# Layer 1's second aggregation as four 64x64 tiles in two PSUM banks

## The chip, the cores and the metric

The kernel runs on one core of a Trainium2 chip. The metric is the device time of one execution in microseconds (us), taken as the median of several runs; lower is better. Where a profile is used, it is one execution recorded by the hardware profiler, and its span goes from the first to the last instruction.

## The reference

There are 128 graphs of 128 nodes with 256 features (`x`, 128x128x256) and one adjacency matrix each (`adj`). Two layers follow each other, each with a layer norm and a ReLU in front and a residual sum behind.

Layer 0 mixes the nodes of a graph by two convolutions and by messages over `exp(-dist)`, and joins them in a GRU cell (the gates r, z and n). It is most of the work.

Layer 1 is a graph convolution on the first 25 nodes of each graph. Five groups of these nodes (25, 9, 7, 6 and 6 of them, 53 rows in all, with repeats) each have their own weights:

```
A    = adj[group] + I;  norm = D^-1/2 A D^-1/2
h    = relu(norm @ (x_g @ W1) + b1)       # 256 -> 512
out  = relu(norm @ (h @ W2) + b2)         # 512 -> 256
fused[group] += softmax(fusion_w)[g] * out
```

What is computed here in the second line is called the second aggregation: `norm @ (h W2)` for the 53 rows of a graph, where `norm` is block diagonal over the five groups. All of it is in float32.

## The kernel before, in words

**Stages.** The kernel has three parts in time. Stage A (normalising, transposing, the first convolution, a Fourier transform) and stage B (products per frequency) alternate in two batches up to 680 us. From there stage C does the gates of layer 0 for four graphs at a time (32 steps `q`), and layer 1 runs beside it, behind it by some steps. At the end layer 1's last blocks run alone.

**Order.** Nothing is scheduled by a compiler. The stages are generators that emit instructions and then yield a pair: TensorE time in us that the emitted step is thought to cost, and a delay before the next step of this generator. `Order.run` picks the next generator from the lanes by these numbers and the lanes' weights. So a cost written in a `yield` decides what stands beside what on every engine. Layer 1's lane has two programs at once with weight 0.2: `prepare(blk)` and `block(blk)`, for eight blocks of 16 graphs.

**prepare(blk).** It loads the 25x25 corners of 16 adjacency matrices as `aj` (L960, on SyncE's queue), lets POOL add the identity into `b1` (L965, eight operations), lets VectorE sum the degrees (L970, five reductions), and builds on TensorE and VectorE the normalised matrices: `ac`, 128 partitions by 8 pairs by 64, where partitions 0 to 63 hold one graph of a pair and 64 to 127 the other (L976, L978, L997, L999, L1002, L1003). From `ac` it forms `r4`, which applies the first aggregation (matmul `pr`, L1007, and four copies by quarters of the partitions, L1011). Positions in `r4` and in `aj` fix which of the four graphs of a group sits in which tile.

**block(blk).** For each of its four groups `q` of four graphs, a matmul with `r4` aggregates (L1027). Then `first(g)` and `second(g)` multiply by W1 and W2 (L1044, L1053) into `yz`. The tail of the block has three functions per `q`: `turn(q)` transposes `yz` to `zt` (L1075, copied by ScalarE, L1079), with 64 partitions for each of two graphs and two such pairs side by side; `gather(q)` does the second aggregation (L1087), adds the bias on VectorE (L1089) and applies ReLU on ScalarE (L1090); `fuse(q)` sums the groups with their weights (L1096), adds to the residual (L1098) and stores (L1101, in the last block L1105). They follow each other in a fixed order: turn 0, 1, 2, gather 0, turn 3, gather 1, gather 2, fuse 0, gather 3, fuse 1, 2, 3.

**The gather's tiles.** A matmul with a contraction over 64 rows and 64 output partitions uses a quarter of the 128x128 array. `ac[rows, ...]` is the weight, `zt[rows, a]` the moving operand. Where the operands start (partition 0 or 64) decides the rows of the array, and where the output starts decides the columns. Before, graph `s` of a pair takes rows 64s and also columns 64s: two tiles of the array on its diagonal, for pair `a` = 0 and then for `a` = 1. Both write the one bank `pg2`.

**PSUM.** The pool `ptmp` has five banks and serves layer 1 and the small products of stage C in turn; a tile takes the bank of the tile five allocations earlier and waits until that one has been read. The pool `pgat` has three, for the large products.

**Stage C, as far as needed.** `turn_back` forms `xc` (L720, L723), and VectorE its sums `tc` (L586). The products of the gates are L738 (into `wrz`, `wn`, `wh` tiles); ScalarE copies the first into `u2` (L772); VectorE empties others (L798, L809, L838, L846, L854) and the output transposes (L887); POOL does the last mix (L864 to L867).

Of the kernel before, what the change touches and what calls it, by code (L numbers as in the profile page):

```python
# [9 lines left out]
FP = mybir.dt.float32  # L10
AF = mybir.ActivationFunctionType
ALU = mybir.AluOpType
# [3 lines left out]
B, N, D = 128, 128, 256  # L16
# [3 lines left out]
P = 128  # L20
GB = 4
# [9 lines left out]
SB = 16  # L31
# [7 lines left out]
NR = sum(SIZES)  # L39
NN = 25  # L40
RP = 64
WIDE = 32
# [50 lines left out]
def _constants():  # L93

    row_node = [n for g in GROUPS for n in g]
    row_group = [i for i, g in enumerate(GROUPS) for _ in g]
    fwd, inv, tap = _fourier()
    parts = {
        "ident": np.eye(P),
        "mhalf": np.full((P, 8), -0.5),  # L100
        "fwd": fwd, "tap": tap, "inv": inv,
        "ones2": np.kron(np.eye(2), np.ones((RP, RP))),
        "et": np.zeros((P, 2 * RP)),
        "same": np.zeros((P, RP)),
        "diag": np.zeros((P, RP)),
        "e4": np.zeros((P, P)),
        "s2": np.zeros((P, 2 * WIDE)),
        "grp": np.zeros((P, NG)),
        "sgrp": np.zeros((P, 2 * NG)),
        "grpt": np.zeros((P, P)),  # L110
        "sel": np.zeros((P, P)),
        "emb": np.zeros((P, 12)),
    }

    roles = {0: [(2, 2, 0), (0, 0, 1), (1, 1, 0), (0, 0, 1)],
             1: [(0, 0, -1), (0, 0, 1), (1, 1, 0), (1, 1, 0)],
             2: [(1, 1, 0), (1, 1, 0), (0, 0, -1), (0, 0, 1)]}
    for j in range(GB):
        for role, factors in roles.items():
            for ch in range(3):  # L120
                k = WIDE * j + 3 * role + ch
                parts["sel"][ch, k] = 1
                parts["emb"][k] = np.array(factors).T.reshape(-1)
    for r, (n, g) in enumerate(zip(row_node, row_group)):
        for s in range(2):
            k = s * RP + r
            parts["et"][n, k] = 1
            parts["same"][k, [i for i in range(NR) if row_group[i] == g]] = 1
            parts["diag"][k, r] = 1
            for j in (s, s + 2):  # L130
                parts["e4"][k, j * WIDE + n] = 1
            parts["s2"][k, s * WIDE + n] = 1
            parts["grp"][k, g] = 1
            parts["sgrp"][k, s * NG + g] = 1
            parts["grpt"][g, k] = 1
    at, o = {}, 0
    for name, a in parts.items():
        at[name] = (o, o + a.shape[1])
        o += a.shape[1]
    return np.concatenate(list(parts.values()), 1).astype(np.float32), at  # L140
# [67 lines left out]
def kernel(ctx: ExitStack, tc: tile.TileContext, x, adj, consts, vecs, w_se, conv1_w,  # L208
                    conv2_w, w_msg, b_msg, w_ih, w_hh, W1, W2, b2, fusion_w, out):
    nc = tc.nc  # L210
# [7 lines left out]
    ptmp = ctx.enter_context(tc.tile_pool(name="ptmp", bufs=5, space=PSUM))  # L218
# [38 lines left out]
    s2w = cp.tile([P, 2 * WIDE], FP, name="s2w")  # L257
# [106 lines left out]
    lab, turn = ExitStack(), []  # L364
# [588 lines left out]
    def prepare(blk):  # L953

        while not (blk - 1 in P_DONE and blk - 2 in {-2, *B1_DONE}):
            yield 0.0, 1.0
        pool, pool2, b1 = S["pool"], S["pool2"], S["b1"]
        ac, r4 = S["ac"][blk % 2], S["r4"][blk % 2]
        aj = pool.tile([NN, SB, NN], FP, tag="dd", name=f"aj{blk}")
        nc.sync.dma_start(out=aj, in_=adj[blk * SB:(blk + 1) * SB, :NN, :NN]  # L960
                          .rearrange("b n m -> n b m"))
        yield 0.0, 4.0

        for r, n, w in _runs():
            nc.gpsimd.tensor_tensor(b1[:, :, r:r + w], aj[:, :, n:n + w],  # L965
                                    ident[:NN, None, n:n + w].to_broadcast([NN, SB, w]),
                                    ALU.add)
        dg = pool2.tile([NN, SB, NG], FP, tag="dg", name=f"dg{blk}")
        for g in range(NG):
            nc.vector.reduce_sum(dg[:, :, g], b1[:, :, OFFS[g]:OFFS[g] + SIZES[g]],  # L970
                                 axis=mybir.AxisListType.X)
        yield 0.0, 7.0

        pa = ptmp.tile([P, SB // 2, RP], FP, tag="tmp", name=f"pa{blk}")
        for p in range(SB // 2):
            nc.tensor.matmul(pa[:, p], b1[:, 2 * p:2 * p + 2, :].rearrange("n s r -> n (s r)"),  # L976
                             c("et")[:NN, :RP], start=True, stop=True)
        nc.vector.tensor_mul(ac, pa, c("same")[:, None, :].to_broadcast([P, SB // 2, RP]))  # L978

        pdg = ptmp.tile([P, SB // 2, 2, NG], FP, tag="tmp", name=f"pdg{blk}")  # L980
        nc.tensor.matmul(pdg.rearrange("p a s g -> p (a s g)"), c("et")[:NN],
                         dg.rearrange("n b g -> n (b g)"), start=True, stop=True)
        dsel = pool.tile([P, SB // 2, 2 * NG], FP, tag="dsel", name=f"dsel{blk}")
        nc.vector.tensor_mul(dsel, pdg.rearrange("p a s g -> p a (s g)"),
                             c("sgrp")[:, None, :].to_broadcast([P, SB // 2, 2 * NG]))
        dm = pool.tile([P, SB // 2], FP, tag="dm", name=f"dm{blk}")
        zo = pool.tile([P, SB // 2], FP, tag="zo", name=f"zo{blk}")
        nc.vector.reduce_sum(dm, dsel, axis=mybir.AxisListType.X)
        nc.vector.tensor_scalar(zo, dm, 0.0, None, op0=ALU.is_equal)
        nc.vector.tensor_add(dm, zo, dm)  # L990
        nc.gpsimd.tensor_tensor(dm, dm, c("mhalf"), ALU.pow)
        nc.gpsimd.tensor_mul(zo, zo, dm)
        nc.gpsimd.tensor_sub(dm, dm, zo)
        yield 2.0, 7.0

        dd = pool.tile([P, SB // 2, RP], FP, tag="dd", name=f"dd{blk}")
        nc.vector.tensor_mul(dd, c("diag")[:, None, :].to_broadcast([P, SB // 2, RP]),  # L997
                             dm[:, :, None].to_broadcast([P, SB // 2, RP]))
        nc.vector.tensor_mul(ac, ac, dm[:, :, None].to_broadcast([P, SB // 2, RP]))  # L999
        yield 0.0, 6.0  # L1000
        pg = ptmp.tile([P, SB // 2, RP], FP, tag="tmp", name=f"pg{blk}")
        nc.tensor.matmul(pg, c("ones2"), dd, start=True, stop=True)  # L1002
        nc.vector.tensor_mul(ac, ac, pg)  # L1003
        yield 0.9, 3.0

        pr4 = ptmp.tile([P, QS, 2, RP], FP, tag="tmp", name=f"pr4{blk}")
        nc.tensor.matmul(pr4.rearrange("p q a r -> p (q a) r"), c("e4"), ac,  # L1007
                         start=True, stop=True)
        for j in range(GB):
            s = slice(j * WIDE, (j + 1) * WIDE)  # L1010
            nc.vector.tensor_copy(r4[s, :, j, :], pr4[s, :, j // 2, :NR])  # L1011
        yield 0.9, 1.0
        P_DONE.add(blk)

    def block(blk):
# [64 lines left out]

        def gather(q):
            zt = zts[q]
            pg2 = ptmp.tile([P, 2, D], FP, tag="tmp", name=f"pg2{blk}_{q}")
            for a in range(2):
                for s in range(2):
                    rows = slice(s * RP, (s + 1) * RP)
                    nc.tensor.matmul(pg2[rows, a], ac[rows, 2 * q + a], zt[rows, a],  # L1087
                                     start=True, stop=True)
            nc.vector.tensor_tensor(zt, pg2, b2row[:, None, :].to_broadcast([P, 2, D]), ALU.add)  # L1089
            nc.scalar.activation(zt, zt, AF.Relu)  # L1090

        def fuse(q):
            zt = zts.pop(q)
            pf = ptmp.tile([P, D], FP, tag="tmp", name=f"pfu{blk}_{q}")
            for a in range(2):
                nc.tensor.matmul(pf[a * 2 * WIDE:(a + 1) * 2 * WIDE], s2w, zt[:, a],  # L1096
                                 start=True, stop=True)
            nc.vector.tensor_add(x1[:, q], x1[:, q], pf)  # L1098
            b0 = blk * SB + q * GB
            if blk < NBLK - 1:  # L1100
                nc.gpsimd.dma_start(out=out[b0:b0 + GB, :WIDE], in_=x1[:, q])  # L1101
                return
            for j in range(GB):
                eng = nc.scalar if q == QS - 1 and j % 2 else nc.sync
                eng.dma_start(out=out[b0 + j, :WIDE], in_=x1[j * WIDE:(j + 1) * WIDE, q])  # L1105

        for what, q in ((turn, 0), (turn, 1), (turn, 2), (gather, 0), (turn, 3), (gather, 1),
                        (gather, 2), (fuse, 0), (gather, 3), (fuse, 1), (fuse, 2), (fuse, 3)):
            what(q)
            if (what, q) == (gather, QS - 1):  # L1110
                B1_DONE.add(blk)
            yield {turn: 0.45, gather: 0.9, fuse: 0.5}[what], 0.5
        F_DONE.add(blk)


# [70 lines left out]
```

## Time and profile before

| what | value |
|---|---|
| median of 3 runs | 2072.65 us |
| lowest and highest run | 2071.14 and 2078.92 us |
| profiled execution, first to last instruction | 2070.6 us |
| mean granted TensorE clock | 0.993 |
| TensorE matmuls busy | 2032.3 us |
| VectorE / ScalarE / POOL busy | 1161.9 / 712.7 / 730.1 us |
| gather matmuls (L1087), 256 records | 34.2 us busy |
| gather additions (L1089), 32 | 689 ns each |

The profile gives no time of its own beyond the span. A float32 matmul leaves two records, one for each of its passes; a transpose leaves one. Records of matmuls overlap[...]: the distance from one start to the next says what a matmul costs, not the length of a record. In the groups, the number after "|" is the time in which at least one record of the group runs, then the mean length of one in ns, then the idle time of the engine before it and who ended it. In the timeline, "x8" is eight records that follow each other, and a bracket says how long the engine was idle before and what it waited for.

### The profile page before, as it was taken

What the parts mean: (1) busy time and instruction counts of PE and PEld (TensorE: products, weight loads), DVE (VectorE), ACT (ScalarE), POOL (GpSimd) and SP (SyncE); (2) the same over time, 40 slices, a digit from 0 to 9 for tenths busy, and PEclk for the clock granted to TensorE, in tenths of its full rate; (3) what the DMA queues carried; (4) which work ended last, traced back from release to release, by engine and by line L of the source; (5) the groups of instructions that cost most, each with busy time, mean ns of one, the idle gap of its engine ahead of it and who ended that gap; (6) DMA issues with size and microseconds to landing.
All of it is one profiled execution on the core that took longest, in us unless ns stands there. A gap on an engine that the chain in (4) does not pass through costs nothing.

```text
span 2070.6 us, 31082 instructions
## 1 busy us (share of the span) xinstructions
PE 2032.3 (98%) x11316; PEld 1649.4 (80%) x11316; DVE 1161.9 (56%) x2711; ACT 712.7 (34%) x1611; POOL 730.1 (35%) x898
## 2 busy tenths in 40 slices
PE   7998999999999999999999999999999999999998
PEld 5667888888888788788778787878787888778875
DVE  6774445874433556646654654566456655654542
ACT  4663223444222444233222332232332323323333
POOL 3552665333664123322422243233223323233230
PEclk9999999999999999899999999999999999999999
DMA  9997788545777444223323232322232332323121
GB/s 215 294 284 237 259 273 269 180 153 202 254 257 249 142 125 139 75 75 90 85 62 90 84 83 76 106 79 75 82 93 72 81 96 80 86 77 102 35 74 52
DMA packets 190135, 281.72 MB, mean 136 GB/s; under 512 B 23625, under 2 KB 143374, under 8 KB 189982
## 3 DMA queue, kind: packets, MB, share of 16 engines
q1 hardware_dynamic: 156942, 185.46, 31.4%
q0 software_dynamic: 32656, 93.98, 14.3%
q8 instruction: 90, 1.47, 0.3%
q14 instruction: 63, 0.52, 0.1%
q10 hardware_dynamic: 384, 0.28, 0.1%
HBM read 187.34 MB, written 92.27 MB: 135 GB/s over the span
## 4 chain that ended last, share of the span: by engine, by line
PE 93%; DVE 2%; DMA 2%; POOL 1%; issue 1%; ACT 1%; SPq 0%; DVEq 0%; POOLq 0%; ACTq 0%
PE p L738 42%; PE pa L526 7%; PE pm L630 5%; PE ph L1044 5%; PE pz L1053 5%; PE pc L421 4%; PE pb L526 3%; PE pi L703 3%; PE pf L432 3%; PE px L656 3%; PE pg L1087 2%; PE po L884 1%; PE pc L717 1%; PE pw L474 1%; PE ph L410 1%; PE py L1027 1%
## 5 line engine op out<-in xcount | busy, mean ns | idle before, releaser
L864 POOL TENSOR_TENSOR d<-hTc,r 128x512 f32<-128x512 f32 x64 | 81.9, 1280 | 244.4 <-ACT r L861 233.8
L526 PE MATMUL pa<-wf,X 128*128 128x256 f32 x640 | 152.2, 381 | 0.0
L893 POOL DMA_DIRECT2D out<-xt x128 | 72.0, 569 | 214.5 <-DVE xt L890 211.6
L558 DVE SCALAR_TENSOR_TENSOR y<-pa,kk 128x512 f32<-128x512 f32 x78 | 53.8, 690 | 151.2 <-ACT kk L557 151.1
L753 ACT ACTIVATE z<-z,brz 128x256 f32<-128x256 f32 x128 | 58.1, 501 | 226.7 <-DVE z L810 192.9
L738 PE MATMUL p<-th,wrz 128*128 128x256 f32 x512 | 132.8, 382 | 0.0
L738 PE MATMUL p<-tm,wrz 128*128 128x256 f32 x512 | 132.3, 381 | 0.0
L738 PE MATMUL p<-tc,wrz 128*128 128x256 f32 x512 | 131.5, 379 | 0.0
L526 PEld LDWEIGHTS pa<-wf,X 128*128 128x128 f32 x640 | 118.1, 190 | 16.2 <-issue 2.0
L630 PE MATMUL pm<-wmsg,hT 128*128 128x256 f32 x512 | 123.5, 387 | 0.0
L421 PE MATMUL pc<-c1w,hTa 128*128 128x256 f32 x512 | 121.6, 384 | 1.2 <-ACT hTa L412 1.2
L720 DVE SCALAR_TENSOR_TENSOR xc<-pc,s_bn,hTc 128x256 f32<-128x256 f32 x128 | 53.1, 478 | 123.3 <-PE pc L717 123.3
L1046 ACT ACTIVATE hh<-ph,vec 128x96 f32<-128x96 f32 (+3 forms) x160 | 64.2, 402 | 136.6 <-PE ph L1044 127.0
L630 PEld LDWEIGHTS pm<-wmsg,hT 128*128 128x128 f32 x512 | 97.1, 193 | 16.0 <-ACT kk L557 1.4
L1044 PE MATMUL ph<-yz,w 128*128 128x96 f32 (+3 forms) x640 | 108.4, 322 | 1.0 <-issue 1.0
L421 PEld LDWEIGHTS pc<-c1w,hTa 128*128 128x128 f32 x512 | 94.5, 191 | 18.3 <-DVE h L424 4.8
L738 PEld LDWEIGHTS p<-tm,wrz 128*128 128x128 f32 x512 | 97.9, 191 | 13.5
L1053 PE MATMUL pz<-hh,w 128*128 128x96 f32 (+3 forms) x640 | 107.3, 321 | 0.0
L738 PEld LDWEIGHTS p<-th,wrz 128*128 128x128 f32 x512 | 94.9, 191 | 13.0 <-issue 0.8
L738 PEld LDWEIGHTS p<-tc,wrz 128*128 128x128 f32 x512 | 95.0, 190 | 12.1 <-issue 0.5
L738 PE MATMUL p<-hTc,wrz 128*128 128x256 f32 x384 | 102.9, 391 | 1.6 <-ACT u L772 1.6
L1044 PEld LDWEIGHTS ph<-yz,w 128*128 128x128 f32 x640 | 86.7, 190 | 21.0 <-issue 15.4
(202 smaller groups left out, 4557.1 us busy)
## 6 DMA issues: line engine op xcount, KB each, us to landing
wf<-wfd SPq DMA_DIRECT2D x160, 256.0 KB, 3.5
wfd<-ws POOLq DMA_DIRECT2D x64, 320.0 KB, 9.2
yd<-y POOLq DMA_DIRECT2D x80, 256.0 KB, 4.3
yt<-yd SPq DMA_DIRECT2D x64, 320.0 KB, 5.0
w<-in_W SPq DMA_DIRECT2D x40, 512.0 KB, 3.6
xa<-in_x SPq DMA_DIRECT2D x128, 128.0 KB, 5.5
hTd<-hTa POOLq DMA_DIRECT2D x32, 512.0 KB, 6.6
hT<-hTd SPq DMA_DIRECT2D x32, 512.0 KB, 6.2
```

The costliest lines, as they stand in the source:

```text
L421: nc.tensor.matmul(pc[:, i], hT[:, k, (2 * h + i) * N:(2 * h + i + 1) * N], c1w[:, k], start=(k == 0), stop=(k == 1))
L432: nc.tensor.matmul(pf[:, i, :F * NB], h1[:, 2 * h + i, k * P:(k + 1) * P], fwd, start=True, stop=True)
L526: nc.tensor.matmul(ps, xk(k), WF[f][:, k, s], start=(k == 0), stop=(k == 1))
L630: nc.tensor.matmul(pm[:, i], hT[:, k, j * N:(j + 1) * N], LATE["wmsg"][:, k], start=(k == 0), stop=(k == 1))
L656: nc.tensor.matmul(px[:, dc, i], msgs[h][:, i, dc * P:(dc + 1) * P], aT[:, 2 * h + i], start=True, stop=True)
L703: nc.tensor.matmul(pi[b * 64:(b + 1) * 64], inv[:F], yt[:, b::2], start=True, stop=True)
L738: nc.tensor.matmul(ps[:, m], w[:, i, k, m * P:(m + 1) * P], factor(i, x, t), start=first and j == 0, stop=last and j == len(n) - 1, skip_g ...
L864: nc.gpsimd.tensor_sub(d, hT[:, dc], r[:, dc])
L893: nc.gpsimd.dma_start(out=out[q * GB + j, WIDE:].rearrange("(t n) c -> n t c", n=WIDE), in_=xt[j * WIDE:(j + 1) * WIDE, 1:4])
L1044: nc.tensor.matmul(ph, w1[:, k, m * P:(m + 1) * P], yz[:, k, :, o:o + n], start=(k == 0), stop=(k == 1))
L1046: nc.scalar.activation(hh[:, m], ph, AF.Relu, bias=v("b1", g * 4 + m))
L1053: nc.tensor.matmul(pz, w2[:, g, m, cc * P:(cc + 1) * P], hs[g][:, m], start=(m == 0), stop=(m == 3))
```

## The change

A gather now uses all four 64x64 tiles of the array. Graph `s` of a pair keeps rows 64s, but pair `a` decides the columns, and each `s` has its own bank `pg2[s]`. The result has the graphs of a group in another place: bank `s` holds pairs `a` = 0 and 1 on partitions 0 to 63 and 64 to 127. So the bias is added by two operations of half the size, one per bank, written into `zt[:, s]`, and the fuse reads `zt[:, s]`. For the graphs to leave in the order in which they are stored, `aj` is loaded with graphs 1 and 2 of each group exchanged, by four transfers in place of one, and the table `e4` and the copies into `r4` follow. The cost that a gather's step yields falls from 0.9 to 0.5, and with it the order of layer 1's steps against stage C's changes from block 0's tail on.

```diff
@@ _constants
-            for j in (s, s + 2):
+            for j in (2 * s, 2 * s + 1):
                 parts["e4"][k, j * WIDE + n] = 1
@@ prepare
-        nc.sync.dma_start(out=aj, in_=adj[blk * SB:(blk + 1) * SB, :NN, :NN]
-                          .rearrange("b n m -> n b m"))
+        for i in range(GB):
+            nc.sync.dma_start(out=aj[:, i % 2 * 2 + i // 2::GB],
+                              in_=adj[blk * SB + i:(blk + 1) * SB:GB, :NN, :NN]
+                              .rearrange("b n m -> n b m"))
...
         for j in range(GB):
             s = slice(j * WIDE, (j + 1) * WIDE)
-            nc.vector.tensor_copy(r4[s, :, j, :], pr4[s, :, j // 2, :NR])
+            nc.vector.tensor_copy(r4[s, :, j % 2 * 2 + j // 2, :], pr4[s, :, j % 2, :NR])
@@ block
         def gather(q):
             zt = zts[q]
-            pg2 = ptmp.tile([P, 2, D], FP, tag="tmp", name=f"pg2{blk}_{q}")
+            pg2 = [ptmp.tile([P, D], FP, tag="tmp", name=f"pg2{blk}_{q}_{s}") for s in range(2)]
             for a in range(2):
                 for s in range(2):
                     rows = slice(s * RP, (s + 1) * RP)
-                    nc.tensor.matmul(pg2[rows, a], ac[rows, 2 * q + a], zt[rows, a],
-                                     start=True, stop=True)
-            nc.vector.tensor_tensor(zt, pg2, b2row[:, None, :].to_broadcast([P, 2, D]), ALU.add)
+                    nc.tensor.matmul(pg2[s][a * RP:(a + 1) * RP], ac[rows, 2 * q + a],
+                                     zt[rows, a], start=True, stop=True)
+            for s in range(2):
+                nc.vector.tensor_add(zt[:, s], pg2[s], b2row)
             nc.scalar.activation(zt, zt, AF.Relu)

         def fuse(q):
...
-            for a in range(2):
-                nc.tensor.matmul(pf[a * 2 * WIDE:(a + 1) * 2 * WIDE], s2w, zt[:, a],
+            for s in range(2):
+                nc.tensor.matmul(pf[s * 2 * WIDE:(s + 1) * 2 * WIDE], s2w, zt[:, s],
                                  start=True, stop=True)
...
-            yield {turn: 0.45, gather: 0.9, fuse: 0.5}[what], 0.5
+            yield {turn: 0.45, gather: 0.5, fuse: 0.5}[what], 0.5
```

## The prediction

> **What bounds the kernel.** I read the page first: the busy time by engine and the chain of work that ended last.
>
> ```profile
> PE 2032.3 (98%) x11316; PEld 1649.4 (80%) x11316; DVE 1161.9 (56%) x2711; ACT 712.7 (34%) x1611; POOL 730.1 (35%) x898
> ...
> PE 93%; DVE 2%; DMA 2%; POOL 1%; issue 1%; ACT 1%; SPq 0%; DVEq 0%; POOLq 0%; ACTq 0%
> ```
>
> TensorE is busy 98% of the span and carries 93% of the chain. So TensorE time that disappears in the middle of the kernel comes off the end, unless something that follows TensorE cannot keep up. The next view is the groups by line, for the gather and the addition that empties it:
>
> ```profile
> L1087 PE MATMUL pg<-zt,ac 64*64 64x256 f32 x256 | 34.2, 388 | 0.0
> L1089 DVE TENSOR_TENSOR zt<-pg,b2row 128x512 f32<-128x512 f32 x32 | 22.0, 689 | 12.4 <-PE pg L1087 12.1
> ```
>
> 256 records are two passes of each of 128 matmuls, so 8 records per gather, and 34.2 us is 1.07 us per gather. The timeline of TensorE around the first gather (start, us, what) says how long it keeps the engine:
>
> ```profile
> 951.24 0.59 PE L738 MATMUL p<-tc,wn 128*128 128x256 f32 x2
> 951.76 1.08 PE L1087 MATMUL pg<-zt,ac 64*64 64x256 f32 x8
> 952.77 0.70 PE L738 MATMUL p<-tm,wn 128*128 128x256 f32 x2
> ```
>
> From 951.76 to 952.77 is 1.01 us. In the trace the eight records start in pairs 6 to 7 ns apart, at 951.762, 952.029, 952.245 and 952.461. So two tiles run together, in four steps of 0.216 us (the spacing of all 256-column records), plus 0.15 us for going into and out of the tiling mode. The question is whether four tiles run together. The kernel has two cases of four, in the timelines around 508 and 518 us:
>
> ```profile
> 508.74 0.65 PE L614 MATMUL pse<-hT,wse 128*32 128x128 f32 x16
> 509.32 1.35 PE L630 MATMUL pm<-wmsg,hT 128*128 128x256 f32 x5
> ...
> 518.15 0.50 PE L643 MATMUL pd<-lr 32*128 32x128 f32 x8
> 518.58 0.66 PE L645 MATMUL pd<-cst,adj 128*128 128x128 f32 x4
> ```
>
> Sixteen records of four column tiles take 0.58 us, eight of four row tiles (each in its own bank) 0.43 us. Sixteen one after the other at their 0.109 us would be 1.74 us. Four together works in both directions.
>
> **What the Trainium skill says.** "TensorEngine Tiling (Array Packing)", section "Restrictions and Gotchas": row tiles must not access the same PSUM bank at the same time. Before, the two tiles of a pair are different row tiles in one bank, on different partitions, and still start 7 ns apart; here the measurement decides. After, each row tile has a bank of its own, so this limit is out of play. Same page, "Tiling Modes": changing the tiling mode drains the engine; the trace agrees (the 0.15 us above). "TensorE: Matmul & The Clock Gate", Part 3: tiles run concurrently, about 4 ns apart; the trace has 6 to 7 ns.
>
> **The change part by part.**
>
> *Gather.* Four tiles at a time need two steps: 1.01 - 2 x 0.216 + 2 x 0.0065 (two more staggered starts) = 0.59 us. Saved: 0.42 us a gather. In both orders of TensorE's instructions the tiling mode is entered and left equally often (59 times for the 128x64 tiles, 28 in and 27 out for the 64x64 ones), and matmuls and weight loads are the same in number, so nothing else changes there.
>
> *Where it counts.* Blocks 0 to 5 (24 gathers, 951 to 1977 us) lie between stage C's products, TensorE full: 24 x 0.42 = 10.1 us.
>
> Block 6 (2017 to 2029 us) has no stage C beside it. VectorE there empties a gather (two additions of 0.42 us in place of one of 0.69), then makes four copies of 1.54 us (L1011). The ring of five banks now gives gather 2 the bank of `pr`, which those copies free at about 2020.9, while TensorE is ready at 2020.2. Worked step by step with the durations above, 0.8 of 1.7 us is lost again: gain 0.9 us.
>
> The last block ends otherwise:
>
> ```profile
> 2061.66 6.67 SPq L1105 DMA_DIRECT2D out<-x  x14
> ```
>
> SyncE issues the output in a row without a pause, 0.47 us each, starting when the first fuse is added (2061.63). Only that start can move. After: gather 0 ends at 2057.6, its additions at 2058.56, Relu at 2059.23, then ScalarE's copy of transpose 3 at 2059.75, which frees the bank for fuse 0; its addition, behind those of gather 2, ends at 2060.94. Gain 0.7 of 1.7 us.
>
> *Order.* The changed cost (0.9 to 0.5) moves layer 1 against stage C. In the before kernel one such position cost TensorE 1.65 us; the timeline around 1035 us:
>
> ```profile
> 1035.61 1.75 DVE L999 TENSOR_TENSOR ac<-ac,dm 128x512 f32<-128x512 f32 x1
> ...
> 1037.28 1.49 DVE L586 TENSOR_TENSOR tc<-xc 128x256 f32<-128x256 f32 x1
> ...
> 1039.92 0.60 ACT L772 ACTIVATE u<-p 128x512 f32<-128x512 f32 x1 [4.79 <-POOL z L867]
> ...
> 1040.57 1.13 PE L738 MATMUL p<-hTc,wrz 128*128 128x256 f32 x4 [1.65 <-ACT u L772]
> ```
>
> Block 2's L997 and L999 stand on VectorE between `xc` and its sums `tc`, in the stretch where POOL works too, and everything behind is late. In the new order they come after L838, among the `wn` products, where blocks 3 to 6 have had them without a wait of TensorE. Gain 1.6 us. Its price if the cover there were gone: their 1.6 us.
> Block 2's five reductions (L970) now stand in front of L887 and L798 of one step, behind POOL's six operations of 1.28 us and eight of 0.47. By my count they leave about 3 us to spare before the product that needs the bank L798 frees. Bounds: 0 to 2 us lost; I take 0.3.
>
> *VectorE.* 2 x 0.42 - 0.69 = 0.15 us more per gather, 4.8 us over the run, on an engine busy 56%: hidden. Behind the first addition are the second, then stage C's operations.
>
> *PSUM.* A gather holds two of five banks. Along the new order TensorE asks for such a bank again 3.1 to 5.9 us after the gather's start in blocks 0 to 5. It is free after 0.59 + 0.16 + 0.12 + 0.84 = 1.7 us with VectorE idle; VectorE was up to 0.88 us behind (once 1.77), so 2.6 (3.5). No wait, except perhaps that one.
>
> *Loading `aj`.* Three more issues of 0.34 us on SyncE per block, 8 us in all. Behind them are the loads `hTc` and `xm` for later steps, and `xm` waited for TensorE (378 us of SyncE's waits), so they have room. POOL's additions wait for the last landing: some 1.1 us later for block 0, where VectorE reached the first reduction at 844.65 and POOL had finished at 843.2: 1.4 us of room. If that is gone the rest falls on TensorE, which already waits 2.48 us there (0 to 1.5 us; I take 0.2). Tables, r4's copies and the fuse keep number and shape: nothing.
>
> Sum: 10.1 + 0.9 + 0.7 + 1.6 - 0.3 - 0.2 = 12.8 us. The profiled execution is 2070.6 us from first to last instruction: 2057.8. The median of the runs is 2.05 us above that span, so 2059.9; I say 2060.0 (0.61% less).
>
> **The rivals.**
> (a) *Four together, but the gain is partly eaten*: banks, `aj` or block 2's new place cost 3 to 10 us. For it: only five banks, and the drained blocks already lose 1.8 us. Against: 2.6 us against 3.1. Time 2062 to 2070.
> (b) *The change doesn't do what it says*: 64x64 tiles run only in pairs, as no trace shows four of this shape. Then a gather stays at 1.01 us and only the 1.6 us of order and small costs remain: about 2071. Against: the four column and four row tiles above.
> (c) *Slower, by the banks*: VectorE frees a gather's second bank so late that TensorE stands still at every gather. It decides from a release 3.1 us after the start; to pass +0.5% (10.4 us) the 24 gathers have to lose 12.8 + 10.4 = 23.2 us, 0.97 each, a release at 4.1 us where I find 2.6. At 4.2 us: about 2085.
>
> A measurement of this kernel can tell about 0.5%, 10.4 us, from no change: faster is below 2062.3.
>
> **How the numbers follow.** Likeliest case 0.65 (2056 to 2062.3, its own range), (a) 0.18, (b) 0.11, (c) 0.06. Faster 0.65; same (a) and (b), 0.28, with 0.01 to slower; slower 0.07. The range 2055.5 to 2068 holds the first and most of (a), about 8 in 10, and leaves out (b) and (c).
>
> **What would show it.** In the profile after: the gather's 256 records busy some 20.5 us in place of 34.2, and 0.6 us from the gather to the next instruction; records starting in fours. If they start in twos, (b). No TensorE wait for the `u` copy of L772 near 1035 us. TensorE's waits at the gather and just behind it under 2 us in all, in the last two blocks; if they are spread over all blocks and name the additions, (c). SyncE's last fourteen issues still without a pause. The forecast is wrong above all if TensorE waits for VectorE grow by more than 3 us, or if a stretch at half clock, as at 846 to 852 us, lengthens or appears elsewhere.

## The result and the profile after

| | median of 6 runs, us | lowest and highest | profiled execution, span | mean granted clock |
|---|---|---|---|---|
| before | 2074.98 | 2071.14, 2081.04 | 2070.6 | 0.993 |
| after | 2066.14 | 2061.22, 2066.73 | 2064.7 | 0.991 |

The ratio is 0.9952, 95% interval 0.9935 to 0.9969: about half a per cent faster. The forecast was 2060.0 us, its range 2055.5 to 2068. So the range holds the time, but a part of the gain that was worked out is missing. By the medians 8.8 us came; on the profiled spans 12.8 us were forecast and 5.9 came. The profiled execution of the kernel before was faster than most of its runs, so the spans show a smaller gain than the medians do.

The page of the changed kernel, busy time by engine and shares of the chain of work:

```profile
PE 2023.3 (98%) x11316; PEld 1644.3 (80%) x11316; DVE 1162.7 (56%) x2743; ACT 712.5 (35%) x1611; POOL 729.1 (35%) x898
...
PE 93%; DVE 3%; DMA 2%; SPq 1%; issue 1%; ACT 0%; POOL 0%; DVEq 0%; ACTq 0%
```

TensorE still carries the chain. Its busy time fell by 9.0 us with the same number of instructions. The groups of the gather and of its additions (busy, mean ns of one, idle before):

```profile
L1092 DVE TENSOR_TENSOR zt<-pg,b2row 128x256 f32<-128x256 f32 x64 | 23.8, 416 | 5.5 <-PE pg L1089 5.5
L1089 PE MATMUL pg<-zt,ac 64*64 64x256 f32 x256 | 21.2, 401 | 0.0
```

The timeline of TensorE around the first gather:

```profile
953.80 0.38 PE L738 MATMUL p<-tc,wn 128*128 128x256 f32 x1
954.11 0.66 PE L1089 MATMUL pg<-zt,ac 64*64 64x256 f32 x8
954.70 0.70 PE L738 MATMUL p<-tm,wn 128*128 128x256 f32 x2
```

From 954.11 to 954.70 is 0.59 us, where it was 1.01. In the trace the records start in fours; over the gathers of blocks 0 to 5 the distance to the next instruction is 0.592 to 0.594 us. The part of the change that was forecast is all there. What took some of it away shows in the granted clock, the share of TensorE's full clock that the chip allowed; in these traces it is 1.00 or 0.50. Here are four stretches of 3.4 us around block 3's `pa` (1265.40 us) in the changed kernel; the columns are the stretch, its length, the busy time and instructions of each engine, then the granted clock, the DMA share and GB/s:

```profile
1260.90:1264.30 3.40, 3.40 (x12) 1.94 (x11) 0.89 (x2) 0.00 (x0) 0.00 (x0) 1.00 0.04 13
1264.50:1267.90 3.40, 3.40 (x25) 2.90 (x24) 1.47 (x3) 0.00 (x0) 0.00 (x0) 0.99 0.00 0
1267.90:1271.30 3.40, 3.40 (x15) 3.13 (x14) 2.39 (x8) 0.56 (x2) 2.06 (x3) 0.50 0.00 0
1271.40:1274.80 3.40, 3.40 (x28) 3.30 (x27) 0.73 (x2) 0.76 (x3) 0.00 (x0) 1.00 0.34 122
```

In the third TensorE ran at half clock. Nothing waited: TensorE is busy for all of 3.40 us in each. The counts of records (x) can't be compared, since the stretches hold matmuls of different lengths; what half clock does to the same instructions is seen under e1. The kernel before has no half clock here. The timeline of TensorE in the changed kernel at this place:

```profile
1265.40 1.99 PE L978 MATMUL pa<-cst,b 25*128 25x64 f32 x16
1267.23 0.40 PE L983 MATMUL pdg<-dg,cst 25*128 25x80 f32 x2
1267.56 0.96 PE L738 MATMUL p<-tm,wn 128*128 128x256 f32 x2
1268.31 1.06 PE L738 MATMUL p<-tc,wn 128*128 128x256 f32 x2
1269.17 2.96 PE L1046 MATMUL ph<-yz,w 128*128 128x112 f32 x16
```

The last matmuls ahead of the stretch are those of `pa` in `prepare` (L976 before, L978 after): sixteen records with a contraction over 25 rows and 64 columns streamed. Reading the clock records of both traces for stretches at 0.5, behind stage C's start:

| | behind block 0's `pa` | behind later `pa` |
|---|---|---|
| before | 858.9 us | none |
| after | 861.7 us | 1267.9, 1858.4, 1998.3 us, 3.41 us each |

Both also have 10.24 us from 845 (848) us, and one at the very end. In each trace the clock changes only at times that are whole multiples of 3.413 us apart; such a period is called a window below.

So where did the time go? The starts of stage C's steps cut the run into segments, here their lengths in us (the fourth column is experiment e1 below, which has no half clock behind any `pa`):

| steps | before | after | e1 | after less before |
|---|---|---|---|---|
| start to 0 | 681.38 | 683.23 | 684.21 | +1.85 |
| 0 to 4 | 166.92 | 167.06 | 167.06 | +0.14 |
| 4 to 5 | 68.23 | 68.59 | 66.77 | +0.36 |
| 5 to 8 | 112.04 | 112.66 | 112.71 | +0.62 |
| 8 to 12 | 163.19 | 160.08 | 160.07 | -3.11 |
| 12 to 16 | 160.64 | 161.17 | 159.51 | +0.53 |
| 16 to 20 | 162.72 | 160.67 | 160.68 | -2.05 |
| 20 to 24 | 156.74 | 155.07 | 155.08 | -1.67 |
| 24 to 28 | 147.61 | 145.94 | 145.93 | -1.67 |
| 28 to 31 | 125.86 | 127.08 | 125.44 | +1.22 |
| 31 to end | 125.24 | 123.13 | 121.48 | -2.11 |

The pure case is steps 20 to 28: 1.67 us less for every four gathers, 0.42 each, to the hundredth what was worked out. In the three segments with a new half-clock stretch the changed kernel is 1.66, 1.64 and 1.65 us longer than e1; in all others from step 0 on, but for 4 to 5 with block 0's `pa`, the two agree within 0.05. Between steps 5 and 20 the new order also moves pieces of layer 1 across the borders of the segments, so these four rows are read as a sum: 4.0 us less, 5.7 without the stretch. From step 0 to the end the sum is -7.7 us; the +1.85 before step 0 is in code that the change leaves alone.

### The profile page after: what moved, and what is told of

Same layout as the page of the kernel before. It is cut to its first block, busy times and chain, and to the rows that moved or that the text cites. A ratio compares the mean times of both kernels' runs of the same rounds, so it can differ in the third digit from the quotient of the medians.

```text
span 2064.7 us, 31168 instructions
## 1 busy us (share of the span) xinstructions
PE 2023.3 (98%) x11316; PEld 1644.3 (80%) x11316; DVE 1162.7 (56%) x2743; ACT 712.5 (35%) x1611; POOL 729.1 (35%) x898
## 4 chain that ended last, share of the span: by engine, by line
PE 93%; DVE 3%; DMA 2%; SPq 1%; issue 1%; ACT 0%; POOL 0%; DVEq 0%; ACTq 0%
PE p L738 43%; PE pa L526 7%; PE pm L630 5%; PE ph L1046 5%; PE pz L1055 5%; PE pc L421 4%; PE pb L526 3%; PE pi L703 3%; PE pf L432 3%; PE px L656 3%; PE pc L717 1%; PE po L884 1%; PE pw L474 1%; PE py L1029 1%; PE ph L410 1%; DMA xa<-in_x 1%
## 5 line engine op out<-in xcount | busy, mean ns | idle before, releaser
L738 PE MATMUL p<-th,wrz 128*128 128x256 f32 x512 | 132.9, 382 | 0.0
L738 PE MATMUL p<-tm,wrz 128*128 128x256 f32 x512 | 132.3, 381 | 0.0
L738 PE MATMUL p<-tc,wrz 128*128 128x256 f32 x512 | 131.5, 379 | 0.0
L738 PEld LDWEIGHTS p<-tm,wrz 128*128 128x128 f32 x512 | 97.9, 191 | 13.5
L1046 PEld LDWEIGHTS ph<-yz,w 128*128 128x128 f32 x640 | 90.1, 197 | 21.3 <-issue 16.5
L738 PEld LDWEIGHTS p<-th,wrz 128*128 128x128 f32 x512 | 94.8, 191 | 12.6 <-issue 1.0
L738 PEld LDWEIGHTS p<-tc,wrz 128*128 128x128 f32 x512 | 95.1, 190 | 11.8
L738 PE MATMUL p<-hTc,wrz 128*128 128x256 f32 x384 | 102.9, 391 | 0.0
```

The lines of the kernel that those rows point to most:

```text
L738: nc.tensor.matmul(ps[:, m], w[:, i, k, m * P:(m + 1) * P], factor(i, x, t), start=first and j == 0, stop=last and j == len(n) - 1, skip_g ...
L1046: nc.tensor.matmul(ph, w1[:, k, m * P:(m + 1) * P], yz[:, k, :, o:o + n], start=(k == 0), stop=(k == 1))
```

## The experiments

All use the line numbers of the changed kernel where nothing else is said. "Step 0 to end" is from stage C's first step to the last instruction of the profiled execution; the start of stage C differs between executions (below), so this is the better measure of a change.

### e1: `pa` with 128 columns streamed

The suspicion was that `pa` is too thin for the clock. Here it streams all 128 columns of `et`, into two banks. Half of its result isn't used; all that follows is computed as in the changed kernel.

```diff
-        pa = ptmp.tile([P, SB // 2, RP], ...)
-        for p in range(SB // 2):
-            nc.tensor.matmul(pa[:, p], b1[:, 2 * p:2 * p + 2, :]..., c("et")[:NN, :RP], ...)
-        nc.vector.tensor_mul(ac, pa, ...)
+        for h in range(2):
+            pa = ptmp.tile([P, SB // 4, 2 * RP], ...)
+            for i in range(SB // 4):
+                p = h * (SB // 4) + i
+                nc.tensor.matmul(pa[:, i], b1[:, 2 * p:2 * p + 2, :]..., c("et")[:NN], ...)
+            nc.vector.tensor_mul(ac[:, h * (SB // 4):(h + 1) * (SB // 4)], pa[:, :, :RP], ...)
```

> The changed kernel, with the eight pa matmuls of prepare reading 128 columns of et in place of 64 (the second half of the result is not used), in two banks, and emptied by two VectorE operations in place of one. TensorE streams twice the columns in the same 1.84 us[...]. Theory A (the half-clock stretches of 3.41 us come from pa's thin streaming when it falls into the first microsecond of a clock window): no half-clock stretch right behind pa, so none between 870 us and the last block, and about 5.3 us less than the changed kernel (three stretches of 1.75 us), a span near 2059. Theory B (the new gather or the new order brings them): about three such stretches stay, and the span stays at 2064 to 2066.

Measured: 2060.56 us (2056.98 to 2062.47, 6 runs), ratio to before 0.993 (0.9914 to 0.9946); step 0 to end 1374.7 us where the changed kernel has 1381.45. No half clock behind any of the eight `pa`. The timeline of TensorE in e1 at the same place:

```profile
1264.60 2.05 PE L980 MATMUL pa<-cst,b 25*128 25x128 f32 x16
1266.49 0.34 PE L986 MATMUL pdg<-dg,cst 25*128 25x80 f32 x2
1266.76 0.70 PE L738 MATMUL p<-tm,wn 128*128 128x256 f32 x2
1267.29 0.59 PE L738 MATMUL p<-tc,wn 128*128 128x256 f32 x2
1267.73 1.95 PE L1049 MATMUL ph<-yz,w 128*128 128x112 f32 x16
```

Twice the columns make `pa` 0.06 us longer, and what follows runs faster: from the second pair of L738 to `ph` it is 0.44 us in place of 0.86, and the sixteen records of `ph` take 1.95 us in place of 2.96. Block 3's `pa` started 2.86 us into its window here, where even the thin one has no stretch behind it, so this place alone shows only what full clock looks like; the proof is in the 28 wide `pa` counted under e9 to e12.

### e2: `pa` with 128 rows contracted

The other way to make it less thin: `b1` gets 128 partitions (the added rows are zero) and the matmul contracts over all of them, still with 64 columns.

```diff
-        S["b1"] = pool.tile([NN, SB, RP], FP, name="b1")
+        S["b1"] = pool.tile([P, SB, RP], FP, name="b1")
...
-                             c("et")[:NN, :RP], start=True, stop=True)
+                             c("et")[:, :RP], start=True, stop=True)
```

> The changed kernel, with pa contracting over all 128 partitions in place of 25, the added rows being zero; streamed columns stay 64. If the clock is let down by few rows in use, the half-clock stretches behind pa vanish as with the wider pa (span near 2059). If by few streamed columns, they stay wherever pa begins less than about 1 us into a 3.41 us window: of eight, two to four, span 2062 to 2066.

Measured: 2062.54 us (2058.53 to 2064.66, 4 runs), ratio 0.9945 (0.9924 to 0.9967), step 0 to end 1374.1. No half clock behind any `pa`, though four of the eight start in the part of a window (0.07 to 0.85 us from its start) where the thin `pa` always has one behind it. Zeros do as well as data. So it isn't the number of columns or of instructions alone: the rows in use count too.

### e3 and e4: the tiles without the order, the order without the tiles

```diff
e3, from the changed kernel
-            yield {turn: 0.45, gather: 0.5, fuse: 0.5}[what], 0.5
+            yield {turn: 0.45, gather: 0.9, fuse: 0.5}[what], 0.5
e4, from the kernel before
-            yield {turn: 0.45, gather: 0.9, fuse: 0.5}[what], 0.5
+            yield {turn: 0.45, gather: 0.5, fuse: 0.5}[what], 0.5
```

> The changed kernel with the gather's yield at 0.9, so that all stands in the order of before. Theory A: the gather alone gives 24 x 0.42 + 1.2 + 1.2 = 12.5 us; the wait of 1.65 us for the u copy near 1035 us is back and the new 1.5 us of waits near 1025 us is gone; half-clock stretches behind pa occur by where pa falls in its window, two or three of eight, 1.75 us each: 7 to 12.5 us below the kernel before in a profile without any. Theory B, in the form that the order brings the stretches: none behind pa, the full 12.5 us. In the form that the four-tile gather brings them: three or more stay.

> The kernel before with the gather's yield at 0.5: the order of the changed kernel, with the old gather. Theory A: -2.1 us (wait near 1035 us gone) +1.5 us (waits for the L846 and L854 additions near 1025 us), so within 1 us of the kernel before, plus 1.75 us for every half-clock stretch behind pa that its window position brings. Theory B (order): three stretches, 4.5 us slower than before.

Measured: e3 2070.18 us (2061.33 to 2075.77, 14 runs), ratio 0.9973 (0.9959 to 0.9987), step 0 to end 1384.7. e4 2075.86 (2071.23 to 2081.87, 14 runs), ratio 1.0009 (0.9998 to 1.002), step 0 to end 1390.7. The profile of e3 seems to say that the new order is worth some 3 us. It isn't so: e3's profile has half clock behind six of its eight `pa` (at 865.5, 1032.8 for two windows, 1275.1, 1473.1, 1671.1 and 2005.6 us), against four in the changed kernel. e4 has it behind two, one more than the kernel before; without that one, 1.65 us, it is 1389.0 us from step 0 to the end, where the kernel before has 1389.2. The order moves `pa` by fractions of a window, and that hides what the order itself does.

### e5: the kernel before with the wide `pa`

The edit of e1, made to the kernel before.

> The kernel before with the wide pa (128 streamed columns in two banks, as in the first experiment), nothing else changed. With theory A it has no half-clock stretch behind pa either, so this pair (before and after, both with wide pa) shows the change without the clock's lottery. The kernel before loses some 2.4 stretches on average (eight pa, each caught in about 1.05 of 3.41 us), 4.2 us: 2071. Against the changed kernel with wide pa (2060.6) that leaves 10 to 11 us of the change itself: 10.1 + 1.2 + 1.2 (gathers) + 2.1 (wait near 1035 us gone) - 1.5 (new waits near 1025 us) = 13.1, less what the load of aj may cost. If the prediction's sum was wrong in the gathers and not by the clock, the pair differs by 7 us or less.

Measured: 2075.87 us (2070.55 to 2084.62, 14 runs), ratio 1.0005 (0.9993 to 1.0017). The median misses the expectation. In the profile no `pa` has half clock behind it, and step 0 to end is 1387.75 us, 1.4 less than before. Between the profiles of e5 and e1 the change can be seen alone: 1387.75 - 1374.73 = 13.0 us. The medians differ by more, 15.3 us, because e5's times fall into two groups (see e9 to e12).

### e6: `aj` by four transfers

From e5, in plain order of the graphs:

```diff
-        nc.sync.dma_start(out=aj, in_=adj[blk * SB:(blk + 1) * SB, :NN, :NN]...)
+        for i in range(GB):
+            nc.sync.dma_start(out=aj[:, i::GB], in_=adj[blk * SB + i:(blk + 1) * SB:GB, :NN, :NN]...)
```

> The kernel before with the wide pa, and aj loaded by four transfers (graphs in the order of before). If the transfers are hidden: as the kernel before with wide pa, within 1 us. If they are what is missing from the sum: 1 to 3 us slower, with POOL's additions near 840 us later and TensorE's wait of 2.5 us there longer.

Measured: 2072.69 us (2066.71 to 2078.39, 22 runs), ratio 0.9982 (0.9972 to 0.9991), step 0 to end 1384.3. Three more issues per block cost nothing that can be seen. The 3.4 us less in the profile are a shorter half-clock stretch at 848 us (3.41 in place of 10.24 us). The four transfers alone don't bring it, as the changed kernel has them and the long stretch too. The median also lies 3.2 us below e5's, and the intervals don't overlap; why this kernel has less half clock isn't shown.

### e7: wide `pa`, tiles, order of before

The edit of e3, made to e1.

> The changed kernel with the wide pa and the gather's yield at 0.9: the gather alone, in the order of before. The wait of 1.65 us near 1035 us is back, the waits near 1025 us (1.5 us) are gone: 0.6 us above the changed kernel with wide pa (2060.6), so 2061.2, and 12.5 us below the kernel before with wide pa. If the order as such matters more than these two waits, it is off by over 2 us.

Measured: 2060.95 us (2056.36 to 2063.87, 6 runs), ratio 0.993 (0.9914 to 0.9947), step 0 to end 1374.85. Against e1 (1374.73) the order is worth 0.1 us, against e5 the tiles are worth 12.9. The waits of TensorE (in total, times, longest) say why, first in e7 and then in e1, which has the new order:

```profile
PE p L738 <- DVE r L854: 2.8, 2, 2.5
...
PE p L738 <- ACT u L772: 1.4, 1, 1.4
...
PE p L738 <- DVE r L846: 0.8, 1, 0.8
```

```profile
PE p L738 <- DVE r L854: 3.4, 3, 2.5
...
PE p L738 <- DVE r L846: 1.2, 2, 0.8
```

In e7 the `u` copy's wait is back, and of the waits for L854 and L846 one each is gone: the two near 1028 us that the new order brought.

### e8: fewer stores at the end

From e1: the last block's first three groups leave by one transfer each in place of four.

```diff
+            if q < QS - 1:
+                nc.sync.dma_start(out=out[b0:b0 + GB, :WIDE], in_=x1[:, q])
+                return
             for j in range(GB):
-                eng = nc.scalar if q == QS - 1 and j % 2 else nc.sync
+                eng = nc.scalar if j % 2 else nc.sync
```

> The changed kernel with the wide pa, and in the last block one store per group for the first three groups in place of four (the last group keeps its four). SyncE then issues 5 in place of 14, so the end follows the last addition (2.8 us after SyncE's first issue) and not SyncE's row of 6.5 us. If SyncE's row sets the end: 2 us less than the changed kernel with wide pa, 2058.5. If the landing of the larger stores sets it: no gain or a loss of up to 1 us.

Measured: 2061.44 us (2056.75 to 2065.86, 6 runs), ratio 0.9933 (0.9914 to 0.9952), the same as e1; from step 31 to the end 121.6 us against 121.5. SyncE's row of issues is gone and the end stays 5.8 to 5.9 us behind the last addition (2049.09 to 2054.97 us; before 2064.74 to 2070.57). So the row isn't the only thing that sets the end. The packets of the larger stores last until 2053.10 us in e8, 3.1 us behind the last issue, where in e1 they end 0.8 us behind it (2057.49): what the shorter row saves, the landing takes.

### e9 to e12: is it luck?

Windows that run free of the kernel could make the three stretches an accident of one execution. So the kernels before and after were profiled once more, and the kernel of e5 twice more.

> The kernel before, unchanged, profiled a second time. If the half-clock stretches behind pa are decided by where pa falls in a window of the clock, this execution differs from the first in their number n: the time from stage C's first step to the end is then 1387.5 + 1.75 n us, and each stretch belongs to a pa that starts within 1.1 us of the start of its window of 3413 ns. If they belong to the kernel's order of work instead, they come where the first profile has them, none behind the later blocks' pa, and that time is 1389.2 as there.

> The changed kernel, unchanged, profiled a second time. By the windows: another number of half-clock stretches than the four behind pa of the first profile (one in the first block, three later), from stage C's first step to the end 1374.7 + 1.75 n us with n their number there (1381.5 in the first profile), each behind a pa that starts within 1.1 us of the start of its window. If the change itself brings them: again at 1268, 1858 and 1998 us, and 1381.5 us.

> The kernel before with pa streaming 128 columns, profiled a second time; half of pa's result isn't used, the rest is computed as before. It should show no stretch behind any pa and 1387.8 us from stage C's first step to the end, as in its first profile. Its times lie in two groups, near 2072 and near 2078. If what parts them is in the work ahead of stage C, a slow execution starts stage C at 687 instead of 681 us and has the same 1387.8 us after it; if it is in stage C, that time grows instead.

> The same kernel as the run before it, profiled a third time, to have more than one start of stage C to compare: 681 us and 1387.8 us after it, or 687 us and the same, if the two groups of times are made ahead of stage C; 681 and about 1393 if they are made in it. No stretch of half clock behind any pa in either case.

Measured:

| | us | step 0 starts | step 0 to end | half clock behind `pa` |
|---|---|---|---|---|
| before, first | | 681.38 | 1389.19 | 858.9 |
| e9, before again | 2074.84 | 683.63 | 1389.43 | 861.6 |
| after, first | 2066.48 | 683.23 | 1381.45 | 861.7, 1267.9, 1858.4, 1998.3 |
| e10, after again | 2065.84 | 682.57 | 1381.47 | 861.0, 1267.1, 1857.7, 1997.6 |
| e5 | 2070.55 | 681.02 | 1387.75 | none |
| e11, e5 again | 2072.25 | 682.76 | 1387.68 | none |
| e12, e5 a third time | 2069.82 | 680.11 | 1387.94 | none |

The expectation that another execution would have another number missed: before and after repeat their stretches, at the same places of the program. Yet the windows explain where. In each trace all changes of the clock lie within 3 ns of one phase of a period of 3413.33 ns. In the six traces with the thin `pa` (before, after, e3, e4, e9, e10) there are 48 `pa`. The 18 that start 0.02 to 1.06 us behind the start of a window are all followed by a stretch at half clock, from the start of the next window. The 30 that start at 1.30 to 3.17 us have none. Of 56 wide ones (e1, e5 to e8, e11, e12) 28 start within 1.06 us, and none is followed by one. From `pa`'s first record to the product behind `pdg` it is 2.16 us (1265.40 to 1267.56), so with a start up to 1.25 us into a window (3.41 - 2.16, an estimate) all of these small matmuls fall into one window. The border found, between 1.06 and 1.30, lies there. That a window must hold them all is a reading that no run tests.

One of the 28 is block 3's in e11, 0.92 us into its window:

```profile
1266.60:1270.00 3.40, 3.40 (x25) 2.91 (x24) 2.82 (x7) 0.00 (x0) 0.00 (x0) 1.00 0.01 2
1270.00:1273.30 3.30, 3.30 (x25) 3.12 (x24) 1.10 (x5) 1.41 (x4) 2.06 (x3) 1.00 0.00 0
```

That is the kernel before with `pa` at 1267.45 us; in the changed kernel the thin one, 0.95 us into its window, brought the 0.50 shown above.

Why the places repeat can be read from the same offsets. The long stretch at 845 us ends with a window, and from its end block 0's `pa` is 0.9 us away in before and e9, 0.6 in the changed kernel, so that it falls 0.4 to 1.0 us into a window in all these traces. From there to block 3's `pa` it is 411.42 and 411.40 us in the two traces of before, which is 120 windows and 1.8 us; after, it is 406.57 and 406.58 us, 119 windows and 0.4 us. So the kernel before had its later `pa` at 2.8 to 1.3 us of a window by its own timing, and the gain itself moved three of them into the first microsecond.

Two profiles of a kernel don't speak for all of its executions. With each time of the changed kernel, of e1 to e8 and of the kernel before beside them, the mean granted clock is on record too, in steps of 0.001, which is about 2 us. At half clock about half of the time is lost, so span x (1 - clock) is an estimate of what it cost a run. Means over the runs, in us:

| kernel | runs | span | lost to the clock | rest |
|---|---|---|---|---|
| before, beside e1 to e4 | 27 | 2073.3 | 14.6 | 2058.7 |
| before, beside e5 to e8 | 35 | 2074.4 | 15.2 | 2059.3 |
| e4 | 14 | 2074.6 | 16.5 | 2058.2 |
| e5 | 14 | 2074.2 | 14.5 | 2059.7 |
| e6 | 22 | 2070.6 | 12.3 | 2058.3 |
| after | 6 | 2063.7 | 17.9 | 2045.8 |
| e1 | 6 | 2058.2 | 11.0 | 2047.3 |
| e2 | 4 | 2060.3 | 16.0 | 2044.3 |
| e3 | 14 | 2067.8 | 22.9 | 2044.9 |
| e7 | 6 | 2059.0 | 12.0 | 2047.0 |
| e8 | 6 | 2059.5 | 12.4 | 2047.2 |

Without the clock's part the kernels with the old gather lie at 2058 to 2060 us and those with four tiles at 2044 to 2047: some 13 us apart, as the profiles of e5 and e1 are. The changed kernel loses some 3 us more to the clock than the kernel before. Its six runs all record 0.991 or 0.992, so it may well repeat its stretches. But not every kernel does: in e3's fourteen runs the clock goes from 0.991 (span 2059.5 us) to 0.986 (2074.0 us), 18 to 29 us lost.

The same record parts the two groups of e5's times. The seven runs of the lower group have a mean clock of 0.9943 and lose 11.8 us, the seven of the upper one 0.9917 and 17.2 us; that is 5.4 of the 6.7 us between the groups. Where in the kernel the upper group loses it stays open, since all three profiles belong to the lower one. These three differ by 2.4 us, and by the table this lies ahead of step 0 (680.1 to 682.8 us). Over all profiles of this study that start ranges from 680.1 to 687.8 us.

## Why the prediction was right and wrong

**Gather, 24 x 0.42 = 10.1 us: right.** Saved 0.419 each, 1.67 per four.

**Block 6 (0.9) and the last block (0.7): right in kind, too small.** From block 6's first transpose to the next `ph` it is 12.12 us in place of 13.37, 1.25 us less; from the last block's second transpose to the end 13.72 in place of 14.96, 1.2 less. One term was wrong in a way that can be seen on VectorE's timeline of the changed kernel: additions that follow each other overlap, so a pair takes 0.76 us and not 2 x 0.42, and four 1.42.

```profile
2053.08 0.76 DVE L1092 TENSOR_TENSOR zt<-pg,b2row 128x256 f32<-128x256 f32 x2 [2.19 <-PE pg L1089]
2054.26 1.42 DVE L1092 TENSOR_TENSOR zt<-pg,b2row 128x256 f32<-128x256 f32 x4 [0.42 <-PE pg L1089]
```

SyncE's row starts 5.1 us after the last block's second transpose, where it was 6.1, and is without a pause as it was, 14 issues:

```profile
2056.03 6.40 SPq L1108 DMA_DIRECT2D out<-x  x14
```

The row as the reason ("Only that start can move") doesn't hold, by e8.

**Order, 1.6 us for the `u` copy: it came, and was given back next door.** The copy follows the product at once now. These lines are from the timeline of the changed kernel:

```profile
1040.43 1.03 PE L738 MATMUL p<-xc,wrz 128*128 128x256 f32 x4
...
1041.55 0.60 ACT L772 ACTIVATE u<-p 128x512 f32<-128x512 f32 x1 [1.45 <-PE p L738]
```

TensorE's wait for it, 1.65 us, is off the list. But the prediction said that L997 and L999 of block 2 would find cover "among the `wn` products, where blocks 3 to 6 have had them without a wait of TensorE". They did not:

```profile
1024.44 0.69 DVE L999 TENSOR_TENSOR dd<-cst,dm 128x512 f32<-128x512 f32 x1
...
1025.04 0.69 DVE L1001 TENSOR_TENSOR ac<-ac,dm 128x512 f32<-128x512 f32 x1
...
1027.43 0.41 DVE L846 TENSOR_TENSOR r<-r,p 128x256 f32<-128x256 f32 x1
...
1027.90 0.70 PE L738 MATMUL p<-tm,wn 128*128 128x256 f32 x2 [0.39 <-DVE r L846]
...
1029.16 0.41 DVE L854 TENSOR_TENSOR r<-r,p 128x256 f32<-128x256 f32 x1
...
1029.62 0.70 PE L738 MATMUL p<-xm,wn 128*128 128x256 f32 x2 [0.59 <-DVE r L854]
```

In blocks 3 to 6 layer 1's own products (`ph`, `pz`) stand between the `wn` products and give VectorE time. In block 2 none do: the same neighbours on VectorE, but not on TensorE. The two operations are short here, 0.69 us each, where in the old place beside POOL's work they took 1.20 and 1.75; still the additions that empty the banks come late by them. The two products start 0.98 and 1.19 us after those ahead of them, where 0.43 is usual, and keep TensorE 0.1 us longer each: 1.5 us lost, where the price had been put at 1.6 us if the cover was gone. e7 confirms the balance: order as such 0.1 us. So the cover is the one step of the sum that failed in its mechanism.

**PSUM, VectorE: right.** In blocks 0 to 5 no wait of TensorE names the gather's additions; they were done 1.5 to 2.7 us after the gather's start (once 3.6), against a need put at 3.1 us or later. **Block 2's reductions, 0.3, and `aj`, 0.2: nothing was seen.** From 850 to 1977 us TensorE's matmuls wait only for the two additions above (0.4 and 0.6 us), and e6 shows no cost of the loads.

**The sum: right without the clock, in part by luck.** Without half clock behind `pa` the change gives 13.0 us from step 0 to the end (e5 to e1); 12.8 had been worked out. The order was put 1.5 us too high, blocks 6 and 7 together 0.9 too low, and 0.5 was taken off for costs that didn't show; these errors nearly cancel. What failed was the step from this sum to the time, which took the granted clock as unchanged. The prediction did name it as what would make it wrong: "if a stretch at half clock, as at 846 to 852 us, lengthens or appears elsewhere". Three appeared, at 1.65 us each: 4.95 us; and that behind block 0's `pa`, which both kernels have, costs 0.4 us more than before. 13.0 - 4.95 - 0.4 = 7.65 us is, to 0.1, the 7.74 that the profiles show from step 0 to the end; with 1.85 us lost ahead of step 0, by an execution that started stage C later, 5.9 are left. The Trainium skill's page "TensorE: Matmul & The Clock Gate", Part 1, gives the window as 3413 ns and free-running, not reset when a kernel starts. The traces agree: 3413.33 ns, and its phase against the first instruction differs between the two profiles of the kernel before (2.20 and 1.41 us). The page puts half clock down to an idle window; here TensorE is recorded busy for 3.40 of 3.40 us, and the measurement decides.

**The rivals.** Four tiles do run together, so (b) falls. No bank holds up the gathers of blocks 0 to 5, so (c) falls. The time lies in the range of (a), 2062 to 2070, and outside that of the likeliest case, but not by (a)'s reasons: of banks, `aj` and block 2's new place only the last cost anything, 1.5 us. So that the range of the forecast, which took in most of (a), holds the time is partly luck.

## What to carry to other kernels

A gain on TensorE moves all that follows against the windows of its clock, so part of it can be lost at places that the change doesn't touch: compare the granted clock of both traces, stretch by stretch, before any wait is blamed. Where a stretch at half clock follows a run of small matmuls and not an idle time, fill the array there, with rows of zeros or columns that nobody reads; here that was worth 5.6 us on the median (2066.14 to 2060.56, in separate comparisons whose intervals overlap a little, 0.9935 to 0.9969 and 0.9914 to 0.9946) and 6.7 us from step 0 to the end. In the kernel before, which had only one such stretch, the same edit left the median where it was (2075.87 us, ratio 1.0005). And cover that one block has for an operation isn't proof for another: look at what stands between the two on the engine that would have to wait.

## What the runs showed of the hardware

- Sixteen fp32 matmul records over 25 rows and 64 columns, 1.83 us in all, are followed by half clock for one window (once two, in e3) if they start within 1.06 us of a window's start (18 of 18), and by none from 1.30 us on (0 of 30). With 128 columns, or with 128 rows, none (0 of 28, and 0 of 4, in the same part of a window). What exactly is counted stays open: more rows alone or more columns alone each prevent it.
- Such a window costs 1.64 to 1.66 us in TensorE's stretches, just under half of its 3.41 us, since what runs in it advances at half speed (a pair of L738 takes 0.86 us in it and 0.44 in e1).
- Columns cost almost nothing in so short a matmul: with 128 in place of 64 the sixteen records took 1.89 us in place of 1.83.
- Additions of 128x256 on VectorE that don't depend on each other start 0.34 us apart though each is recorded for 0.41 us.
- From stage C's start on, the profiled executions of one kernel agree within 0.3 us in 1380 (before 1389.19 and 1389.43, after 1381.45 and 1381.47, e5 1387.68 to 1387.94). What these differ in otherwise lies in the 680 us ahead, in code that the change leaves alone; what it is there stays open.
- Between runs of one kernel most of the spread goes with the granted clock: e3 from 0.991 at a span of 2059.5 us to 0.986 at 2074.0 us, e5's two groups 0.9943 and 0.9917.
